# One float32r copy of the FFN weights, read in float16 through its upper halves

## The chip, the cores and the metric

The kernel runs on one core of one Trainium2 chip. The metric is the device time of one launch in microseconds (us). The kernel before was run three times; its median is 608.09 us (607.62 to 609.0).

## The reference

The input `x` has 8 batches of 512 tokens with 256 features. It is normalised, and then goes two ways: through attention with 16 heads of 16 features, rotary positions and a window of 250 tokens, and through a feed-forward network (FFN) whose weights are plus or minus one. The product of both is added to `x`.

```python
def _conn_dense(kernel_bool, x):
    w = jnp.where(kernel_bool, jnp.float32(1.0), jnp.float32(-1.0))
    return x @ w
...
h = jnp.concatenate([x, -x], axis=-1)
h = s0 * _conn_dense(k0, h)          # (512, 1024) booleans
h = jax.nn.relu(h) * 2
h = s1 * _conn_dense(k1, h)          # (1024, 1024) booleans
h = jax.nn.relu(h) * 2
h = s2 * _conn_dense(k2, h)          # (1024, 256) booleans
...
xn = _layernorm(x, axis=-1)
s = _L0_attn_ref(xn, L0_attn_in_proj_w, L0_attn_out_proj_w)
g = _silu(_L0_ffn_ref(xn, ...))
x = x + s * g
```

The first layer sees `x` and `-x`, so its two halves of weights fold into their difference, which is -2, 0 or 2 (in the kernel before, half of that: -1, 0 or 1).

## The kernel before

**Tiling.** Everything stands transposed: features on the 128 partitions, the 512 tokens of a batch along the free dimension. The 8 batches follow each other. In each, the FFN's first layer makes 8 tiles of 128 features from 2 chunks of input, the second makes 8 tiles from 8 chunks, the last makes 2 tiles from 8 chunks. Attention runs in 9 steps a batch, spread among the FFN's matmuls.

**Two parts of each activation.** Activations keep nearly float32's precision in two parts: `hi` is the value rounded to float16 (ScalarE, L307, L346, L529) and `lo` is what is left over, as float32r (VectorE, L305, L347, L527). A layer multiplies the weights with both and adds up in PSUM: first all chunks in float16, then all chunks in float32r (`of_both`, L514). For this the weights lie in SBUF twice, `w0`, `w1`, `w2` each with a part "h" (float16) and a part "l" (float32r), L158 to L164.

**Making the weights.** At the start the booleans come in as bytes (`kb0`, `kb1`, `kb2`). `make_w0h` subtracts the halves of `k0` (VectorE, L183), `make_w0l` copies that to float32r (ScalarE, L186), `make_w1` turns a slice of 128 output columns of `k1` into plus or minus a constant for one part (L188 to L194), on ScalarE or GpSimd. The constants carry the sign of the scale `s1`. `make_w2` does both parts on GpSimd (L196). The sizes of the three scales and the constants of the two powers of two are put right once at the end (`scales`, L200 to L207).

**Order.** The order of the work on each engine is written by hand. `everything` (L992) is a list of (time, cost, function); `run` (L226) sorts it by that planned time and issues the instructions so. Functions may return followers with a delay. Each engine then works through its instructions in that order and waits on semaphores for what it needs. The times of the weight slices stand in L1004 to L1010. DMA copies are issued from SP's queue, a few at the start from ScalarE's.

**q and k.** For the scores, q and k are projected, rotated (`rotate`, GpSimd, L425), split in a high half (ScalarE, L442) and a low half (VectorE, L449), written to DRAM (L435) and read back stacked (`stack`, L457). The scores are L733, their exponentials L752 (ScalarE), the masks L768 and L775 (GpSimd), the values L807. From batch 1 on the normalised `x` is made in transposed form: the moments go through DRAM (L281, L290), VectorE applies them (L301), ScalarE makes the high part `xh` (L307).

**Where weights are read.** `layer` (L502), with its matmul at L518, and `last` (L554), with its matmul at L572. A float16 matmul is two instructions on TensorE, a weight load and the matmul; a float32 or float32r one loads its weights itself, which shows as a load in the trace too.

The scale constants, and the reads in `layer`:

```python
X_SCALE, W1_SCALE = 2.0 ** 7, 2.0 ** -10
...
of_both = [(p, c) for p in "hl" for c in range(nc_in)]
...
    p, c = of_both[k]
    nc.tensor.matmul(
        ph, w[p][:, c, ts(f, P)], st[src + p][:, c, cols],
        start=(k == 0), stop=(k == n - 1),
    )
```

`plain_ffn` and all that stands under `tc.If(found < n_rows, label="general")` is a second way for inputs that the fast way can't take (a row with hardly any variance, a sum of exponentials out of range). It isn't entered with these inputs.

Of the kernel before, what the change touches and what calls it, by code (L numbers as in the profile page):

```python
# [23 lines left out]

LEAST, MOST = 1e-20, 1e30

LEAST_VAR = 1e-11

X_SCALE, W1_SCALE = 2.0 ** 7, 2.0 ** -10


@with_exitstack
def tile_attention_times_gated_ffn(
# [42 lines left out]
    nc = tc.nc  # L78
    P = 128
# [4 lines left out]
    EC = E // P  # L84
    F0, F1 = k0.shape[1], k1.shape[1]
# [7 lines left out]
    const = ctx.enter_context(tc.tile_pool(name="const", bufs=1))  # L93
# [23 lines left out]
    raw_pool = raw.enter_context(tc.tile_pool(name="raw", bufs=1))  # L117
# [11 lines left out]
    for n in (1, 0, 2):  # L129
# [26 lines left out]


    w0, w1, w2 = (  # L158
        {
            p: const.tile(shape, dt, name=f"w{i}{p}_sb")  # L160
            for p, dt in (("h", F16), ("l", F32R))
        }
        for i, shape in enumerate(([P, EC, F0], [P, NF0, F1], [P, NF1, E]))
    )  # L164

    sgn = const.tile([P, 3], F32, name="sgn")
    sgnx = const.tile([P, 1], F32, name="sgnx")
    sgn2 = const.tile([P, 3], F32, name="sgn2")
    sgnn = const.tile([P, 3], F32, name="sgnn")
# [15 lines left out]
    def make_w0l(c):  # L185
        nc.scalar.copy(w0["l"][:, c], w0["h"][:, c])  # L186

    def make_w1(f, p, engine):  # L188

        w, k = w1[p][:, :, ts(f, P)], kb1[:, :, ts(f, P)]  # L190
        if engine is nc.scalar:
            nc.scalar.activation(w, k, AF.Identity, bias=sgnn[:, 1:2], scale=sgn2[:, 1:2])
        else:
            engine.tensor_scalar(w, k, sgn2[:, 1:2], sgnn[:, 1:2], ALU.mult, ALU.add)  # L194

    def make_w2():  # L196
        for p in "hl":
            nc.gpsimd.tensor_scalar(w2[p], kb2, 2.0, -1.0, ALU.mult, ALU.add)

        mag = small.tile([P, 3], F32, tag="mag", name="mag")  # L200
        nc.vector.tensor_tensor(mag, s_sb[:, 0:3], sgn, ALU.mult)
        nc.vector.tensor_scalar(
            mag[:, 0:1], mag[:, 0:1], 8.0 / (X_SCALE * W1_SCALE), mag[:, 1:2],
            ALU.mult, ALU.mult,
        )
        nc.vector.tensor_tensor(scales[:, 0:1], mag[:, 0:1], s_sb[:, 2:3], ALU.mult)
        nc.vector.tensor_scalar(scales[:, 1:2], scales[:, 0:1], -1.0, None, ALU.mult)  # L207
# [294 lines left out]
    def layer(b, name, src, w, f, part=0, parts_=1, cols=slice(0, T)):  # L502

        st = states[b]
        nc_in = w["l"].shape[1]
        if f == 0 and part == 0 and cols.start == 0:
            for p, dt in (("h", F16), ("l", F32R)):
                st[name + p] = hpool.tile(
                    [P, NF0, T], dt, tag=f"{name}{p}", name=f"{name}{p}_{b}"
                )  # L510
        if part == 0:
            st["h"] = ps_m.tile([P, T], F32, tag="mm", name=f"h_ps_{b}_{f}")
        ph = st["h"][:, cols]
        of_both = [(p, c) for p in "hl" for c in range(nc_in)]  # L514
        n = len(of_both)
        for k in range(n * part // parts_, n * (part + 1) // parts_):
            p, c = of_both[k]
            nc.tensor.matmul(  # L518
                ph, w[p][:, c, ts(f, P)], st[src + p][:, c, cols],
                start=(k == 0), stop=(k == n - 1),  # L520
            )
# [32 lines left out]
    def last(b, u, how):  # L554
        st = states[b]
        f, cols = outputs(b)[u]
        if how == "final":
            pz = ps_s.tile([P, 2, T], F32, tag="sc", name=f"z_ps_{b}_{u}")[:, 0, : T // 2]
        else:
            pz = ps_m.tile([P, T], F32, tag="mm", name=f"z_ps_{b}_{u}")  # L560
            if b + 1 == B:
                pz = pz[:, : T // 2]
        if how == "at once":
            for c in range(NF1):
                nc.tensor.matmul(
                    pz, w2["l"][:, c, ts(f, P)].bitcast(F32), st["h2p"][:, c, cols],
                    start=(c == 0), stop=(c == NF1 - 1),
                )
        else:
            for p in "hl":  # L570
                for c in range(NF1):
                    nc.tensor.matmul(  # L572
                        pz, w2[p][:, c, ts(f, P)], st["h2" + p][:, c, cols],
                        start=(c == 0 and p == "h"), stop=(c == NF1 - 1 and p == "l"),
                    )
        if cols.start == 0:
            st["gate of", f] = outs.tile([P, T], F32, tag=f"gate{f}", name=f"gate_{b}_{f}")
        gate = st["gate", u] = st["gate of", f][:, cols]
        if how == "final":
            residual(b, u)  # L580
# [12 lines left out]

            return [(0.0, ends)]

        def scale():
            nc.vector.tensor_scalar(gate, pz, scales[:, 0:1], None, ALU.mult)
            if how != "later":
                return [(7.5 if u == 0 else 11.0, lambda: gate_ready(b, u))]

        return [(0.0, scale)]

    def plain_ffn(b):

        st = states[b]
        for name, src, w in (("h1p", "xp", w0["l"]), ("h2p", "h1p", w1["l"])):
# [391 lines left out]
    ]  # L998
    for c in range(EC):
        everything += [  # L1000
            (-34.4 if c == 0 else -32.8, 0, lambda c=c: make_w0h(c)),
            (-32.9 if c == 0 else -32.6, 0, lambda c=c: make_w0l(c)),
        ]
    for w, f, at, engine in (  # L1004
        ("l", 0, 4.6, nc.gpsimd), ("l", 1, 4.65, nc.gpsimd), ("l", 2, 10.2, nc.gpsimd),
        ("h", 0, -17, nc.scalar), ("h", 1, 8.6, nc.scalar), ("h", 2, 10.3, nc.gpsimd),
        ("l", 3, 11.8, nc.gpsimd), ("l", 4, 11.9, nc.gpsimd), ("l", 5, 12.0, nc.gpsimd),
        ("l", 6, 19.3, nc.gpsimd), ("l", 7, 19.4, nc.gpsimd), ("h", 3, 15.2, nc.scalar),
        ("h", 4, 17.0, nc.scalar), ("h", 5, 18.7, nc.scalar), ("h", 6, 20.4, nc.scalar),
        ("h", 7, 22.2, nc.scalar),  # L1010
    ):
        everything.append((at, 0, lambda f=f, w=w, e=engine: make_w1(f, w, e)))
    for b in range(B):
        everything += prepare(b) + ffn(b)
        for u in range(len(outputs(b))):
# [138 lines left out]
```

## Time and profile before

| what | us |
|---|---|
| median of 3 runs | 608.09 |
| the profiled execution | 606.75 |
| its span, first to last instruction | 605.0 |
| TensorE busy | 595.0 |
| VectorE busy | 382.6 |
| GpSimd busy | 310.6 |
| ScalarE busy | 294.6 |
| weight loads on TensorE (beside its matmuls) | 367.4 |

The busy shares by stage, in the answer by windows, one row a stretch:

```profile
core 0: us, PE busy (x) PEld busy (x) DVE busy (x) ACT busy (x) POOL busy (x), PEclk, DMA share, GB/s
0.00:15.00 15.00, 11.67 (x49) 9.40 (x50) 9.84 (x31) 6.04 (x11) 3.68 (x12) 1.00 0.86 267
15.00:40.00 25.00, 24.59 (x135) 15.49 (x137) 19.01 (x35) 19.15 (x27) 24.18 (x19) 1.00 0.67 233
40.00:60.00 20.00, 19.80 (x168) 9.77 (x160) 9.84 (x14) 11.44 (x14) 10.52 (x15) 1.00 0.24 84
60.00:80.00 20.00, 19.84 (x196) 11.88 (x188) 11.21 (x16) 11.68 (x14) 9.32 (x15) 1.00 0.78 273
80.00:200.00 120.00, 120.00 (x872) 71.19 (x871) 76.01 (x123) 58.55 (x81) 56.00 (x69) 1.00 0.30 99
```

A row gives the stretch, its length, then the busy time and number of instructions of TensorE's matmuls (PE), its weight loads (PEld), VectorE (DVE), ScalarE (ACT) and GpSimd (POOL), the granted TensorE clock, the busy share of the DMA engines and what they moved. From 15 to 40 us GpSimd is busy for 24.18 of 25 us and ScalarE for 19.15; there the weights are made. From 80 us on TensorE has a matmul in flight all the time. In groups of instructions, "L518 PEld LDWEIGHTS ... x576 | 51.2, 98" means: 576 weight loads of line 518, 51.2 us in all, 98 ns each on average. Matmuls are pipelined: one starts before the one ahead has ended, so the pace is read from starts, not from durations.

### The profile page before, as it was taken

How to read it: one execution, taken by the hardware profiler on the slowest of the kernel's cores; microseconds unless marked ns; L12 is line 12 of the kernel's file. 1: busy time of each engine (PE TensorE's matmuls, PEld its weight loads, DVE VectorE, ACT ScalarE, POOL GpSimd, SP SyncE). 2: the span in 40 equal slices, each digit the busy share in tenths (PEclk: the TensorE clock that was granted, in tenths of full speed). 3: DMA queues.
4: the chain of work that ended last, by engine and by line, in shares of the span. 5: the costliest groups of instructions: out<-in, count | busy, mean ns of one | idle time of the engine just before them, and what ended most of it. 6: DMA issues, size and time to landing. Idle time of an engine off the chain costs nothing. (4 is left out here: it accounts for less than half of the span.)

```text
span 605.0 us, 11181 instructions
## 1 busy us (share of the span) xinstructions
PE 595.0 (98%) x4492; PEld 367.4 (61%) x4492; DVE 382.6 (63%) x606; ACT 294.6 (49%) x414; POOL 310.6 (51%) x368
## 2 busy tenths in 40 slices
PE   7999999999999999999999999999999999999996
PEld 6654566555665556556566566655565556667785
DVE  6854647557576485665856658566676566645665
ACT  3776664444554535545354454543554435554422
POOL 2975532456623664436635457245572356536743
PEclk9999999999999999999999999999999999999998
DMA  8562822226331353315333252432524216212201
GB/s 268 219 192 87 280 88 89 87 83 231 106 120 56 134 180 105 123 53 205 109 105 123 92 211 75 145 110 85 209 91 135 89 70 224 91 53 71 89 1 38
DMA packets 38056, 74.46 MB, mean 123 GB/s; under 512 B 5360, under 2 KB 13040, under 8 KB 38000
## 3 DMA queue, kind: packets, MB, share of 16 engines
q1 hardware_dynamic: 35568, 71.48, 34.4%
q10 hardware_dynamic: 2432, 2.23, 1.2%
q8 instruction: 36, 0.59, 0.4%
q14 instruction: 20, 0.16, 0.1%
HBM read 44.30 MB, written 29.39 MB: 122 GB/s over the span
## 5 line engine op out<-in xcount | busy, mean ns | idle before, releaser
L752 ACT ACTIVATE p<-sc 128x1024 f32<-128x1024 f32 (+2 forms) x144 | 138.3, 1012 | 74.8 <-PE sc L733 44.9
L768 POOL TENSOR_SCALAR_AFFINE_SELECT p<-p 128x512 f32<-128x512 f32 x128 | 92.4, 727 | 126.3 <-ACT p L752 126.3
L518 PE MATMUL h_ps<-h1l,w1l_sb 128*128 128x512 f32 (+1 forms) x576 | 146.3, 396 | 0.0
L518 PE MATMUL h_ps<-h1h,w1h_sb 128*128 128x512 f16 (+1 forms) x576 | 123.1, 357 | 0.0
L518 PEld LDWEIGHTS h_ps<-h1l,w1l_sb 128*128 128x128 f32 x576 | 100.3, 188 | 29.4 <-issue 9.2
L529 ACT ACTIVATE h2h<-h_ps 128x512 f16<-128x512 f32 (+1 forms) x72 | 39.4, 548 | 113.2 <-PE h_ps L518 113.2
L518 PEld LDWEIGHTS <-w1h_sb 128*128 128x128 f16 x576 | 51.2, 98 | 58.8 <-issue 17.5
L775 POOL TENSOR_SCALAR_AFFINE_SELECT p<-p 128x512 f32<-128x512 f32 (+1 forms) x96 | 49.3, 514 | 72.6 <-ACT p L752 69.2
L807 PE MATMUL po<-p,v_pad 128*32 128x378 f32 (+4 forms) x1216 | 76.7, 372 | 0.1
L633 DVE RECIPROCAL den<-den 128x256 f32<-128x256 f32 (+1 forms) x32 | 52.5, 1644 | 24.9 <-POOL den L628 24.9
L527 DVE SCALAR_TENSOR_TENSOR h2l<-h_ps,h2h 128x512 fp32r<-128x512 f32 (+1 forms) x72 | 43.7, 608 | 30.5 <-ACT h2h L529 30.5
L733 PEld LDWEIGHTS sc<-q,k 32*128 32x128 f32 x1216 | 44.2, 184 | 30.4 <-issue 21.5
L527 DVE SCALAR_TENSOR_TENSOR h1l<-h_ps,h1h 128x512 fp32r<-128x512 f32 x64 | 42.7, 679 | 25.7 <-ACT h1h L529 25.6
L733 PE MATMUL sc<-q,k 32*128 32x378 f32 (+4 forms) x1216 | 58.1, 307 | 0.5 <-DMA q<-dq 0.3
L884 DVE RECIPROCAL S<-S 128x128 f32<-128x128 f32 x64 | 57.5, 920 | 0.1
L518 PE MATMUL h_ps<-xl,w0l_sb 128*128 128x512 f32 x128 | 52.3, 489 | 0.0
L807 PEld LDWEIGHTS po<-p,v_pad 128*32 128x32 f32 x1216 | 31.8, 109 | 28.7 <-issue 17.0
L529 ACT ACTIVATE h1h<-h_ps 128x512 f16<-128x512 f32 x64 | 38.0, 598 | 18.3 <-PE h_ps L518 18.3
L301 DVE TENSOR_TENSOR xT<-xT,of_all 128x512 f32<-128x512 f32 x28 | 22.1, 794 | 28.5 <-DMA of_all<-d 28.0
L518 PE MATMUL h_ps<-xh,w0h_sb 128*128 128x512 f16 x128 | 38.5, 382 | 0.1
L572 PE MATMUL z_ps<-h2l,w2l_sb 128*128 128x512 f32 (+1 forms) x144 | 36.1, 391 | 0.2 <-DVE h2l L527 0.2
L425 POOL TENSOR_TENSOR m_ka<-m_ka,m_kb 128x512 f32<-128x512 f32 x16 | 20.1, 1275 | 28.4 <-DVE m_kb L404 28.4
(101 smaller groups left out, 734.8 us busy)
## 6 DMA issues: line engine op xcount, KB each, us to landing
q<-dq SPq DMA_DIRECT2D x64, 256.0 KB, 3.3
dq<-qh SPq DMA_DIRECT2D x16, 512.0 KB, 3.1
dq<-m_qa SPq DMA_DIRECT2D x16, 512.0 KB, 5.3
k<-dk SPq DMA_DIRECT2D x32, 256.0 KB, 2.7
dk<-kh SPq DMA_DIRECT2D x8, 512.0 KB, 2.6
dk<-m_ka SPq DMA_DIRECT2D x8, 512.0 KB, 2.8
x<-in_x_dram SPq DMA_DIRECT2D x30, 128.0 KB, 2.9
xT<-in_x_t_dram SPq DMA_DIRECT2D x7, 512.0 KB, 5.5
```

Source lines behind the costliest of these rows:

```text
L301: nc.vector.tensor_tensor(xT, xT, st["of_all"][:, i], op)
L518: nc.tensor.matmul(ph, w[p][:, c, ts(f, P)], st[src + p][:, c, cols], start=(k == 0), stop=(k == n - 1),)
L527: nc.vector.scalar_tensor_tensor(lo, ph, 0.0, hi, ALU.max, ALU.subtract)
L529: high = lambda: nc.scalar.activation(hi, ph, AF.Relu)
L572: nc.tensor.matmul(pz, w2[p][:, c, ts(f, P)], st["h2" + p][:, c, cols], start=(c == 0 and p == "h"), stop=(c == NF1 - 1 and p == "l"),)
L633: nc.vector.reciprocal(part, part)
L733: nc.tensor.matmul(sc[r // 2][:, r % 2, ds(off, n)], st["k0", g][row, ts(j, P)], st[f"q{turn}", g][row, ds(j * P + first, n)], start=(turn ...
L752: nc.scalar.activation(p[:, 2 * half : 2 * half + 2, :n], sc[half][:, :, :n], AF.Exp, scale=D ** -0.5,)
L768: nc.gpsimd.affine_select(out=block, in_=block, compare_op=ALU.is_ge, fill=0.0, base=0, pattern=[[0, 4], [1, P]], channel_multiplier=-1,)
L775: nc.gpsimd.affine_select(out=block, in_=block, compare_op=ALU.is_ge, fill=0.0, base=-1, pattern=[[0, 4], [-1, beyond]], channel_multiplier=1,
L807: nc.tensor.matmul(po[32 * r : 32 * r + 32, ds(j * P + first, n)], v_columns(j, g, r), p_[:, r, ds(off, n)], start=(j == 0), stop=(done an ...
L884: nc.vector.reciprocal(part, part)
```

## The change

The weights are kept once, as float32r, with the values -2, 0 and 2. A float32 number of this size has zeros in its lower 16 bits, and its upper 16 bits read as float16 give the same number (2.0 is 0x40000000 in float32 and 0x4000 in float16). So the float16 matmuls read the float32r tile as a float16 tile of twice the width, and of it every second element: a view with a step of 2 elements (4 bytes) where the float16 copy had a step of 1.

With it:
- `make_kd0` (VectorE, in the place of `make_w0h`) writes the difference of `k0`'s halves to a float16 tile `kd0` in the pool of raw inputs; `make_w0` (ScalarE, in the place of `make_w0l`) writes it times two to `w0`.
- `make_w1` makes one slice for each f, 8 in place of 16. On ScalarE these are f = 0, 2, 6, 7 (before: 7 float16 slices), on GpSimd f = 1, 3, 4, 5 (before: 8 float32r slices and 1 float16 slice).
- `make_w2` makes one tile in place of two.
- Constants: `X_SCALE` is 2^-5 in place of 2^7, the scale of `w1` is 2 in place of 2^-10, and `LEAST_VAR`, the smallest variance that the fast way takes, 1e-7 in place of 1e-11.

In the built program TensorE, VectorE and SP have the same instructions in the same order as before, apart from tiles, steps and waits. The float16 copies took 24 KB of each partition; the buffers behind them move.

```diff
-X_SCALE, W1_SCALE = 2.0 ** 7, 2.0 ** -10
+X_SCALE = 2.0 ** -5
...
     w0, w1, w2 = (
-        {
-            p: const.tile(shape, dt, name=f"w{i}{p}_sb")
-            for p, dt in (("h", F16), ("l", F32R))
-        }
+        const.tile(shape, F32R, name=f"w{i}_sb")
         for i, shape in enumerate(([P, EC, F0], [P, NF0, F1], [P, NF1, E]))
     )
+
+    def weights(w, p, c, cols):
+        if p == "l":
+            return w[:, c, cols]
+        return w[:, c].bitcast(F16).rearrange("p (f two) -> p f two", two=2)[:, cols, 1]
...
-        nc.vector.tensor_scalar(sgn2, sgn, 2.0 * W1_SCALE, None, ALU.mult)
-        nc.vector.tensor_scalar(sgnn, sgn, -W1_SCALE, None, ALU.mult)
-
-    def make_w0h(c):
-
-        nc.vector.tensor_tensor(w0["h"][:, c], kb0[:, c], kb0[:, EC + c], ALU.subtract)
-
-    def make_w0l(c):
-        nc.scalar.copy(w0["l"][:, c], w0["h"][:, c])
-
-    def make_w1(f, p, engine):
-
-        w, k = w1[p][:, :, ts(f, P)], kb1[:, :, ts(f, P)]
+        nc.vector.tensor_scalar(sgn2, sgn, 4.0, None, ALU.mult)
+        nc.vector.tensor_scalar(sgnn, sgn, -2.0, None, ALU.mult)
+
+    kd0 = raw_pool.tile([P, EC, F0], F16, name="kd0")
+
+    def make_kd0(c):
+
+        nc.vector.tensor_tensor(kd0[:, c], kb0[:, c], kb0[:, EC + c], ALU.subtract)
+
+    def make_w0(c):
+        nc.scalar.mul(w0[:, c], kd0[:, c], 2.0)
+
+    def make_w1(f, engine):
+
+        w, k = w1[:, :, ts(f, P)], kb1[:, :, ts(f, P)]
...
     def make_w2():
-        for p in "hl":
-            nc.gpsimd.tensor_scalar(w2[p], kb2, 2.0, -1.0, ALU.mult, ALU.add)
+        nc.gpsimd.tensor_scalar(w2, kb2, 4.0, -2.0, ALU.mult, ALU.add)
...
-                ph, w[p][:, c, ts(f, P)], st[src + p][:, c, cols],
+                ph, weights(w, p, c, ts(f, P)), st[src + p][:, c, cols],
...
-                        pz, w2[p][:, c, ts(f, P)], st["h2" + p][:, c, cols],
+                        pz, weights(w2, p, c, ts(f, P)), st["h2" + p][:, c, cols],
...
-    for w, f, at, engine in (
-        ("l", 0, 4.6, nc.gpsimd), ("l", 1, 4.65, nc.gpsimd), ("l", 2, 10.2, nc.gpsimd),
-        ("h", 0, -17, nc.scalar), ("h", 1, 8.6, nc.scalar), ("h", 2, 10.3, nc.gpsimd),
-        ("l", 3, 11.8, nc.gpsimd), ("l", 4, 11.9, nc.gpsimd), ("l", 5, 12.0, nc.gpsimd),
-        ("l", 6, 19.3, nc.gpsimd), ("l", 7, 19.4, nc.gpsimd), ("h", 3, 15.2, nc.scalar),
-        ("h", 4, 17.0, nc.scalar), ("h", 5, 18.7, nc.scalar), ("h", 6, 20.4, nc.scalar),
-        ("h", 7, 22.2, nc.scalar),
+    for f, at, engine in (
+        (0, -17, nc.scalar), (1, 4.6, nc.gpsimd), (2, 8.6, nc.scalar),
+        (3, 10.2, nc.gpsimd), (4, 11.8, nc.gpsimd), (5, 11.9, nc.gpsimd),
+        (6, 15.2, nc.scalar), (7, 17.0, nc.scalar),
     ):
```

More of the change, by code (lines that the diff above doesn't have):

```diff
@@ L25 @@
 LEAST, MOST = 1e-20, 1e30
-LEAST_VAR = 1e-11
-X_SCALE, W1_SCALE = 2.0 ** 7, 2.0 ** -10
+LEAST_VAR = 1e-7
+X_SCALE = 2.0 ** -5
 @with_exitstack
@@ L202, in make_w2 @@
         nc.vector.tensor_scalar(
-            mag[:, 0:1], mag[:, 0:1], 8.0 / (X_SCALE * W1_SCALE), mag[:, 1:2],
+            mag[:, 0:1], mag[:, 0:1], 1.0 / X_SCALE, mag[:, 1:2],
             ALU.mult, ALU.mult,
@@ L504, in layer @@
         st = states[b]
-        nc_in = w["l"].shape[1]
+        nc_in = w.shape[1]
         if f == 0 and part == 0 and cols.start == 0:
@@ L565, in last @@
                 nc.tensor.matmul(
-                    pz, w2["l"][:, c, ts(f, P)].bitcast(F32), st["h2p"][:, c, cols],
+                    pz, w2[:, c, ts(f, P)].bitcast(F32), st["h2p"][:, c, cols],
                     start=(c == 0), stop=(c == NF1 - 1),
@@ L605, in plain_ffn @@
         st = states[b]
-        for name, src, w in (("h1p", "xp", w0["l"]), ("h2p", "h1p", w1["l"])):
+        for name, src, w in (("h1p", "xp", w0), ("h2p", "h1p", w1)):
             h = st[name] = hpool.tile(
@@ L1000, in tile_attention_times_gated_ffn @@
         everything += [
-            (-34.4 if c == 0 else -32.8, 0, lambda c=c: make_w0h(c)),
-            (-32.9 if c == 0 else -32.6, 0, lambda c=c: make_w0l(c)),
-        ]
-    for w, f, at, engine in (
-        ("l", 0, 4.6, nc.gpsimd), ("l", 1, 4.65, nc.gpsimd), ("l", 2, 10.2, nc.gpsimd),
-        ("h", 0, -17, nc.scalar), ("h", 1, 8.6, nc.scalar), ("h", 2, 10.3, nc.gpsimd),
-        ("l", 3, 11.8, nc.gpsimd), ("l", 4, 11.9, nc.gpsimd), ("l", 5, 12.0, nc.gpsimd),
-        ("l", 6, 19.3, nc.gpsimd), ("l", 7, 19.4, nc.gpsimd), ("h", 3, 15.2, nc.scalar),
-        ("h", 4, 17.0, nc.scalar), ("h", 5, 18.7, nc.scalar), ("h", 6, 20.4, nc.scalar),
-        ("h", 7, 22.2, nc.scalar),
+            (-34.4 if c == 0 else -32.8, 0, lambda c=c: make_kd0(c)),
+            (-32.9 if c == 0 else -32.6, 0, lambda c=c: make_w0(c)),
+        ]
+    for f, at, engine in (
+        (0, -17, nc.scalar), (1, 4.6, nc.gpsimd), (2, 8.6, nc.scalar),
+        (3, 10.2, nc.gpsimd), (4, 11.8, nc.gpsimd), (5, 11.9, nc.gpsimd),
+        (6, 15.2, nc.scalar), (7, 17.0, nc.scalar),
     ):
-        everything.append((at, 0, lambda f=f, w=w, e=engine: make_w1(f, w, e)))
+        everything.append((at, 0, lambda f=f, e=engine: make_w1(f, e)))
     for b in range(B):
```

## The prediction

> **What bounds the kernel now.** I read the page first (busy shares, then the costliest groups), then the groups of TensorE split by shape, then the timeline around the start and around single weight loads.
>
> ```profile
> PE 595.0 (98%) x4492; PEld 367.4 (61%) x4492; DVE 382.6 (63%) x606; ACT 294.6 (49%) x414; POOL 310.6 (51%) x368
> L518 PEld LDWEIGHTS h_ps<-h1l,w1l_sb 128*128 128x128 f32 x576 | 100.3, 188 | 29.4 <-issue 9.2
> L518 PEld LDWEIGHTS <-w1h_sb 128*128 128x128 f16 x576 | 51.2, 98 | 58.8 <-issue 17.5
> L807 PEld LDWEIGHTS po<-p,v_pad 128*32 128x32 f32 x1216 | 31.8, 109 | 28.7 <-issue 17.0
> ```
>
> TensorE is busy for 595.0 of 605.0 us; no other engine passes 63%. So what shortens another engine's work counts only where TensorE waits for it, and what lengthens TensorE's own pace counts in full. The last three lines are the weight loads in question: 98 ns for 128 float16 columns, 188 ns for 128 columns of 4 bytes, 109 ns for 32 columns of 4 bytes.
>
> ```profile
> L518 PE MATMUL h_ps<-h1h,w1h_sb 128*128 128x512 f16 x448 | 106.4, 381 | 0.0
> L518 PE MATMUL h_ps<-h1h,w1h_sb 128*128 128x256 f16 x128 | 16.7, 274 | 0.0
> ...
> 30.38 1.90 PE L518 MATMUL h_ps<-h1h,w1h_sb 128*128 128x512 f16 x8
> ...
> 114.24 0.55 PEld L518 LDWEIGHTS <-w1h_sb 128*128 128x128 f16 x4 [0.20 <-issue]
> 114.25 0.82 PE L518 MATMUL h_ps<-h1h,w1h_sb 128*128 128x512 f16 x3
> ...
> 580.32 1.05 PE L518 MATMUL h_ps<-h1h,w1h_sb 128*128 128x256 f16 x8
> 581.12 1.18 PE L518 MATMUL h_ps<-h1l,w1l_sb 128*128 128x256 f32 x8
> 582.14 1.05 PE L518 MATMUL h_ps<-h1h,w1h_sb 128*128 128x256 f16 x8
> ```
>
> Eight pipelined matmuls of 381 ns end after 1.90 us, so they start (1.90-0.381)/7 = 0.217 us apart; those of 256 columns (1.05-0.274)/7 = 0.111 us apart. (Row by row, start to start: 216 and 109 ns.) A float16 load of 98 ns fits beside either. Longer loads fit too: from 580.32 to 582.14, eight float16 and eight float32r matmuls take 1.82 us, so the float32r ones are (1.82-8x0.111)/8 = 0.117 us apart although each has a 188 ns load. The record of a load is longer than what it takes from the pace.
>
> The exception is the first load of a group: at 114.24 it starts with its matmul (114.25), not one matmul ahead. Row by row, 114 of the 848 float16 loads (576 at L518 for w1, 128 for w0, 144 at L572) start within 5 ns of their own matmul: the first after float32r or attention matmuls, not after the plain float32 projections. Such a first matmul holds the next one off by 226 ns instead of 216.
>
> The start of the program has the few waits:
>
> ```profile
> 17.98 2.37 POOL L194 TENSOR_SCALAR w1l_sb<-kb,sgn,sgnn 128x1024 fp32r<-128x1024 uint8 x2
> 20.32 3.48 POOL L425 TENSOR_TENSOR m_qa<-m_qa,m_qb 128x512 f32<-128x512 f32 x2
> 23.84 1.05 ACT L442 CAST qh<-m_qa 128x1024 fp32r<-128x1024 f32 x1 [1.07 <-POOL m_qa L425]
> 24.91 1.22 DVE L449 TENSOR_TENSOR m_qa<-m_qa,qh 128x1024 fp32r<-128x1024 f32 x1 [1.43 <-ACT qh L442]
> 34.83 0.62 PE L733 MATMUL sc<-q,k 32*128 32x378 f32 x12 [0.32 <-DMA q<-dq]
> 42.75 2.89 DVE L301 TENSOR_TENSOR xT<-xT,of_all 128x512 f32<-128x512 f32 x4 [2.25 <-DMA of_all<-d]
> 48.74 0.79 PE L733 MATMUL sc<-q,k 32*128 32x378 f32 x14 [0.20 <-ACT p L752]
> ```
>
> Read it as a chain: GpSimd makes two weight slices, then rotates q; ScalarE and VectorE wait for that; their halves go through DRAM; the first scores wait for the stacked q. From 34.07, where the first scores start, to the float16 matmuls at 35.38 is 1.31 us; the same 16 score matmuls take 0.72 us at 59.44. Stall: 0.59. At 48.10 they take 1.40, a stall of 0.68: they wait for ScalarE, whose exponentials stand behind the normalised x of batch 1, which waits for `of_all`, which queues on SP behind the q copies.
>
> [...]188-109 = 79 ns for 96 columns is 0.82 ns a column, so 83 ns of a record are fixed[...]. No row shows the strided form.[...]
>
> **The change, part by part.**
>
> *The steady stream.* The order on TensorE, VectorE and SP is that of before, instruction by instruction; only tiles and wait counts differ. Matmuls, columns and moving operands stay. 848 loads now read every second float16. Bounds: nothing at best (the packed load is the shortest record there is, so no gain), and at worst the 188 ns of a 4-byte load, 90 ns more. [...]about 12 ns more, a record of 110. For the 734 early loads that costs nothing: they start 108 ns (256 columns) or 214 ns (512) ahead, and the 188 ns loads started 115 ns ahead without cost. The 114 late ones pay: 114 x 12 ns = +1.4 us. At 90 ns they would pay 10.3 us.
>
> *w0.* ScalarE doubles a difference (ACTIVATE) where it cast one (CAST, 1.05 us at 10.92 and at 12.76). VectorE's subtraction stays. The float16 matmuls now wait for ScalarE's output, done at 13.81, 1.5 us before their first load at 15.28; up to 0.25 us more each is hidden there. VectorE's `xl` behind it may slip as much, and the rope products after it; the q product that matters runs at 18.05, behind `h1l`. Nothing.
>
> *w1 and w2, ScalarE.* Four slices instead of seven: 3 x 1.23 = 3.7 us less, at 32 to 39 us. The slice at 34.67 stood ahead of the first exponentials, but these need the scores anyway.
>
> *w1 and w2, GpSimd.* Four slices instead of nine and one w2 instead of two: 4 x 1.19 + 2.24 + 1.90 = 8.9 us less. Only one slice (1.19 us) goes from ahead of the q rotation: it starts when `m_qb` is there (VectorE, 18.05 + 1.28 = 19.33) instead of at 20.32, 1.0 us earlier. ScalarE is free by 22.77, so `qh`, VectorE's low half, the copies to and from DRAM all move by 1.0 us, and q lands in time: the stall of 0.59 at 34.07 goes. On SP the copies of the moments and `of_all` follow in the same queue and move by the same 1.0 us; so do the normalisation, ScalarE's two `xh` and the exponentials behind them. At 46.3 the last needs `h2h`, which TensorE gives 0.59 earlier. ScalarE then stands ahead by about 0.8 us at 48.1. What is late next is still ScalarE, so the start gives 0.8 us in all, not 0.59 + 0.68. Bounds: 0.3 (the copies are held by DMA traffic) and 1.6 (both stalls and the odd tenths after them). After 60 us TensorE is the bound, and carries that to the end.
>
> *Readiness of the single copy.* Each slice is now needed at the float16 half, about 1.6 us before the float32r half. On GpSimd f = 3 to 5 follow the rotation and end near 26.5; f = 3 is read at 40.76. On ScalarE f = 7 ends near 32.3 and is read after 70. No slice has under seven us of cover. The four scale constants, the smaller buffers and the new `kd0` (released with the raw booleans, last read before 14 us) cost nothing.
>
> *Sum.* +1.4 - 0.8 = +0.6 us. The profiled execution took 606.75 us, 605.0 of span and 1.75 around it: 607.35. It lies 1.34 under the median of 608.09, so against the median 608.7.
>
> **Rivals.** The smallest difference that a measurement of this kernel can tell from none is about 0.2%, 1.2 us.
>
> *The strided load is as short as the packed.* For: [...]a fixed part of 83 ns may hide the rest.[...] Then only the start moves: 608.09 - 0.8 = 607.3, and 606.5 at its bound.
>
> *The load loses its fast form (the slower side).* The place is the 114 late loads. The price is up to 90 ns each: 10.3 - 0.8 gives 617.6; half of it 612.4. It decides from a record of about 98 + (1.2+0.8)/114 = 116 ns on.[...]
>
> *The moving stream is slowed.* Float32r matmuls of 512 columns run at 0.234 (row by row) where float16 has 0.216, in proportion to their columns (0.117 against 0.109 at 256), so it is their stream that is slow, not their load. Were strided loads to do the same to 688 float16 matmuls of 512 and 160 of 256 columns, that is 688 x 0.018 + 160 x 0.008 = 13.7 us: 621.0. Against it: [...]plain float32 streams that bear 190 ns loads.
>
> **How the numbers follow.** Forecast 0.40 (most of it within 0.2%: same 0.24, slower 0.14, faster 0.02); load free 0.30 (faster 0.20, same 0.10); load slow 0.15; stream slowed 0.07; anything else, such as the moved buffers, 0.08 (half and half). Faster 0.26, same 0.34, slower 0.40. The range of the forecast alone is 606.9 to 610.2; down to 606.4 it takes in the free load with a start worth 1.6, up to 614 the lower half of the slow load. Left out: 0.05 of the slow load, the slowed stream, 0.06 below.
>
> **What would show it.** The float16 load's mean: 110 ns is the forecast, 98 the first rival, 188 the second. Pace of the float16 matmuls inside a group: still 0.216 and 0.109; 0.234 is the third. First matmul of a late group: 238 ns instead of 226. The q rotation on GpSimd near 19.3; the scores near 34 us without a wait for DMA; the next ones near 47 us with a shorter one for ScalarE. Wrong altogether, if TensorE waits anywhere for a weight slice, or if the stalls of the start come back later.

## The result, and the profile after

The changed kernel took 606.06 us (median of 14 runs, 605.48 to 606.77), before in the same session 607.06 (14 runs); the ratio is 0.9979, interval 0.9969 to 0.9989. Two more sessions, below, gave 606.56 beside 607.06 (0.9993, 0.9982 to 1.0004) and 606.32 beside 607.02 (0.9988, 0.9982 to 0.9995). The change makes the kernel about 0.7 us faster, 0.1%: (1.00 + 0.50 + 0.70)/3. The forecast was 608.7, 0.6 us slower. A ratio here is not the quotient of the two medians (it lies nearer to that of the means), so a difference of medians and its ratio can disagree by some hundredths of a per cent, which is as much as some of the effects below.

From the page of after: its line of engines, and three groups of its fifth part.

```profile
PE 594.7 (98%) x4492; PEld 367.3 (61%) x4492; DVE 381.1 (63%) x606; ACT 291.7 (48%) x411; POOL 302.9 (50%) x362
...
L521 PE MATMUL h_ps<-h1h,w_sb 128*128 128x512 f16 (+1 forms) x576 | 123.1, 357 | 0.0
L521 PEld LDWEIGHTS h_ps<-h1l,w_sb 128*128 128x128 f32 x576 | 100.2, 188 | 29.5 <-issue 9.2
L521 PEld LDWEIGHTS <-w_sb 128*128 128x128 f16 x704 | 61.1, 98 | 74.7 <-issue 29.1
```

The work on GpSimd fell to 302.9 us, by 7.7 where 8.9 had been foreseen. The last line settles the largest doubt: the float16 load, which now reads every second value, is still 98 ns long. Row by row the paces (0.216 and 0.109 us) and the time by which the first matmul of a late group holds the next one off (226 to 227 ns) are those of before as well.

The start, from the timelines of after (start, us taken, engine, line, operation, and in brackets what it waited for):

```profile
18.14 1.20 POOL L198 TENSOR_SCALAR w_sb<-kb,sgn,sgnn 128x1024 fp32r<-128x1024 uint8 x1
19.30 3.51 POOL L428 TENSOR_TENSOR m_qa<-m_qa,m_qb 128x512 f32<-128x512 f32 x2
22.83 1.05 ACT L445 CAST qh<-m_qa 128x1024 fp32r<-128x1024 f32 x1
23.91 1.72 SPq L438 DMA_DIRECT2D dq<-qh  x2
25.72 1.22 SPq L438 DMA_DIRECT2D dq<-m_qa  x2
29.79 1.82 SPq L460 DMA_DIRECT2D q<-dq  x2
34.81 0.62 PE L736 MATMUL sc<-q,k 32*128 32x378 f32 x12 [0.27 <-DMA q<-dq]
48.07 1.15 PE L736 MATMUL sc<-q,k 32*128 32x378 f32 x16
```

SP's copies of q in before:

```profile
24.91 0.80 SPq L435 DMA_DIRECT2D dq<-qh  x2
26.16 1.61 SPq L435 DMA_DIRECT2D dq<-m_qa  x2
30.23 2.07 SPq L457 DMA_DIRECT2D q<-dq  x2
```

One slice stands ahead of the q rotation instead of two, and the rotation starts at 19.30 instead of 20.32. SP issues the first store of q (`dq<-qh`) 1.0 us earlier too (23.91; before 24.91). But this issue takes 1.72 us instead of 0.80, the reload `q<-dq` starts only 0.44 us earlier, and the scores wait for q until 34.81, as before (34.83). Counted from TensorE's first matmul of the w0 layer (15.71 in before, 15.87 in after), the first store is issued 1.16 us earlier and the second reload, the one that lands just before those scores start, lands 0.19 us earlier (18.89 instead of 19.08). The rest of the lead, 0.97 us, is lost between that issue and the landing.

To see where the gain arises, the start of the same TensorE matmul is compared in the two traces. Worked out from the records, in us:

```
matmul                         before   after   lead of after
before the w0 layer             15.71   15.87   -0.16
first of the w1 layer           26.79   26.82   -0.03
first scores                    34.07   34.10   -0.03
after the scores of 48.1        49.51   49.19    0.32
scores of 64.5                  64.53   64.19    0.34
behind these                    65.60   65.39    0.21
scores of 69.1                  69.10   68.89    0.21
behind these                    70.04   69.62    0.42
float16 matmuls of 71           70.98   70.39    0.59
one near the end               592.08  591.48    0.60
```

After 71 us nothing moves. The first row is a warning: in the three profiles of after, one unchanged program, TensorE starts the w0 layer at 15.87, 15.59 and 16.50 us, so a single pair of profiles can differ here by as much as the whole gain. The lead comes out of a few waits, and three of them had not been foreseen: it loses 0.13 at 64.5, and gains 0.21 and 0.17 between 69 and 71. Whether each is of the change or of the execution, one profile cannot tell; the experiments had to.

### The profile page after: what moved, and what is told of

Read it like the earlier page. It is cut to its first block, busy times and chain, and to the rows that moved or that the text cites. A ratio compares the mean times of both kernels' runs of the same rounds, so it can differ in the third digit from the quotient of the medians.

```text
span 604.2 us, 11172 instructions
## 1 busy us (share of the span) xinstructions
PE 594.7 (98%) x4492; PEld 367.3 (61%) x4492; DVE 381.1 (63%) x606; ACT 291.7 (48%) x411; POOL 302.9 (50%) x362
## 5 line engine op out<-in xcount | busy, mean ns | idle before, releaser
L521 PE MATMUL h_ps<-h1l,w_sb 128*128 128x512 f32 (+1 forms) x576 | 146.1, 395 | 0.0
L521 PE MATMUL h_ps<-h1h,w_sb 128*128 128x512 f16 (+1 forms) x576 | 123.1, 357 | 0.0
L521 PEld LDWEIGHTS h_ps<-h1l,w_sb 128*128 128x128 f32 x576 | 100.2, 188 | 29.5 <-issue 9.2
L521 PEld LDWEIGHTS <-w_sb 128*128 128x128 f16 x704 | 61.1, 98 | 74.7 <-issue 29.1
L521 PE MATMUL h_ps<-xl,w_sb 128*128 128x512 f32 x128 | 52.3, 489 | 0.0
L521 PE MATMUL h_ps<-xh,w_sb 128*128 128x512 f16 x128 | 38.4, 382 | 0.1
L575 PE MATMUL z_ps<-h2l,w_sb 128*128 128x512 f32 (+1 forms) x144 | 36.0, 391 | 0.2 <-DVE h2l L530 0.2
```

The lines of the kernel that those rows point to most:

```text
L521: nc.tensor.matmul(ph, weights(w, p, c, ts(f, P)), st[src + p][:, c, cols], start=(k == 0), stop=(k == n - 1),)
L575: nc.tensor.matmul(pz, weights(w2, p, c, ts(f, P)), st["h2" + p][:, c, cols], start=(c == 0 and p == "h"), stop=(c == NF1 - 1 and p == "l"),)
```

## The experiments

### The view alone, and the making alone

reads_only keeps both copies and their making; the float16 matmuls read the upper halves of the float32r copy:

```diff
+    def weights(w, p, c, cols):
+        if p == "l":
+            return w["l"][:, c, cols]
+        return w["l"][:, c].bitcast(F16).rearrange("p (f two) -> p f two", two=2)[:, cols, 1]
...
-        nc.scalar.copy(w0["l"][:, c], w0["h"][:, c])
+        nc.scalar.mul(w0["l"][:, c], w0["h"][:, c], 2.0)
```

> Both copies are made in the order of before, by the same engines, with the values of two; the float16 matmuls read the float32r copy by the view, and the float16 copies of w1 and w2 are written and read by nobody. Theory 'start' (the whole gain comes from the fewer weight slices at the start, the view is free): the time of before, a ratio of 0.999 to 1.001; float16 loads 98 ns; TensorE reaches 48.4, 65 and 70 us where before does, within 0.15. Rival 'stream' (the view or the single copy makes the later stream better): a ratio of 0.997 to 0.999 with the start as before.

Measured: 606.99 us, 606.96 beside it, ratio 0.9995 (0.9985 to 1.0004). The group of its loads:

```profile
L523 PEld LDWEIGHTS <-w1l_sb 128*128 128x128 f16 x576 | 51.3, 98 | 58.8 <-issue 17.6
```

98 ns again; from 71 to 560 us it takes 489.10 us, before 489.12. After 71 us, where almost all of these loads stand, the view gives nothing and costs nothing. One expectation missed: TensorE does not reach the named places within 0.15 us of before, but 1.1 us later at 48 us and 0.55 at 65 and 70 us. 0.44 of that is there at its first matmul of the w0 layer (16.15); the rest comes and goes at the waits of 34 and 48 us.

making_only is the reverse: the changed making, with one packed tile as the weights of every float16 matmul.

```diff
+    flat = const.tile([P, P], F16, name="flat")
+    nc.gpsimd.memset(flat, 0.0625)
...
-        return w[:, c].bitcast(F16).rearrange("p (f two) -> p f two", two=2)[:, cols, 1]
+        return flat
```

> The weights are made as in the changed kernel, but every float16 matmul reads one packed tile of 128x128 that is filled once with 0.0625: what is left out is the float16 part's use of the weights. Theory 'start': the time of the changed kernel, a ratio to before of 0.997 to 0.999, loads 98 ns. Rival 'stream': the time of before, 0.999 to 1.001. If packed loads are still cheaper than strided ones where the trace can't show it, this is faster than the changed kernel by up to 1.4 us (114 late loads by 12 ns, the term of the prediction).

606.47 us, ratio 0.9991 (0.9983 to 0.9999), 489.09 us from 71 to 560. The two intervals overlap, so the times alone do not decide; together with the unchanged loads and paces they point to the making, or to what moves with it.

### What a longer load costs

The float16 loads of w1 take every fourth, then every eighth value (the columns are then others than the reference's).

```diff
+        if w is w1:
+            at = 4 * P * (cols.start // P % 4)
+            return w[:, c].bitcast(F16)[:, at + 1 : at + 4 * P : 4]
```

> The 576 float16 loads of w1 read every fourth float16 in place of every second (8 bytes apart), so they take other columns than the reference's. [...]record 98 ns, same time as the changed kernel.[...] 110 or more, and the first matmul of a late group above 226 ns.

> The same with every eighth float16 (16 bytes apart), other columns than the reference's. If distance never counts: 98 ns and the time of the changed kernel. [...]a record of 110 to 190 ns; the early loads still hide, the 76 late ones of w1 pay 1 to 7 us.

From the page of step8, the group that holds w1's 576 loads and w0's 128 ordinary ones:

```profile
L524 PEld LDWEIGHTS <-w_sb 128*128 128x128 f16 x704 | 84.3, 138 | 59.8 <-issue 30.8
```

Row by row, w1's loads are mostly 113 ns in step4 and 143 to 144 in step8, late or not. step4 took 607.34 us (1.0006, 0.9996 to 1.0016), step8 610.01 (1.0044, 1.0027 to 1.0060). In step4 TensorE leads before by 1.11 us at 71 us and by 0.01 at the end, lost in steps of 0.016 us, one at each late load of w1 (63 of the 114 late ones are w1's); in step8 a step is 0.047. Inside a group the paces stay 0.216 and 0.109 us in both. So only the late loads pay, and they pay what their record grows: 16 and 47 ns. That the prediction had right. But growth starts behind step 2: there the record is 98 ns, as for packed weights, and at step 4 it is 15 ns longer. So in both runs the second of the two outcomes named above came.

### Which part of the making

Three versions of after put a part of the removed making back, into tiles that nobody reads, beside after unaltered: one GpSimd slice ahead of the q rotation (slice_ahead), four behind it and a second w2 (behind_back), three ScalarE slices (scalar_back).

```diff
+    spare = const.tile([P, NF0, P], F32R, name="spare")
+    for f, at, engine in ((2, 4.65, nc.gpsimd),):
+        everything.append((at, 0, lambda f=f, e=engine: make_spare(f, e)))
...
+    for f, at, engine in ((5, 18.7, nc.scalar), (6, 20.4, nc.scalar), (7, 22.2, nc.scalar)):
```

> The changed kernel once more, unaltered, beside the three that follow. Both theories: 606.0 us, ratio 0.998. It is here for the spread of the places where before and after differ: in the first profile of after the block of 16 scores at 48.1 us took 1.13 us instead of 1.40, the stretch from 65.6 to 71.0 us was 0.38 us shorter, and the stall at the first scores (34.1 us) was as long as before. What comes again is of the kernel; what does not is of the execution.

> The changed kernel with one more slice of weights made by GpSimd ahead of the q rotation, into a tile that nobody reads, as before had it. Theory 'ahead' (the gain is the q rotation's lead): q rotation back at 20.3 us, the scores at 48.1 us back to 1.40 us, and 0.3 to 1.0 us of the gain of 1.0 gone: 606.4 to 607.0. Rival 'behind' (the gain is in what GpSimd no longer does after the rotation): q rotation back at 20.3 us all the same, the time stays at 606.0 to 606.2, and the stretch from 65.6 to 71.0 us stays 0.38 us shorter than in before.

> The changed kernel with the other GpSimd making put back behind the q rotation: four more slices and a second making of w2, into tiles that nobody reads. Theory 'ahead': the lead of the q rotation is kept (19.3 us), the scores at 48.1 us stay at 1.13 us, the time stays at 606.0 to 606.3. Rival 'behind': the mask of the sixth step waits 0.46 us again, the stretch from 65.6 to 71.0 us is 0.38 us longer, and the time is 606.4 to 607.0.

> The changed kernel with the three slices that ScalarE no longer makes put back at their former places, into a tile that nobody reads: 3.7 us of ScalarE in the first 65 us. Theories 'ahead' and 'behind': nothing comes back, 606.0 to 606.2. A third, 'scalar' (ScalarE's exponentials and evictions of the first steps come earlier because it makes less): the scores at 48.1 us or the stretch from 49 to 65 us grow by 0.2 to 1.0 us, 606.3 to 607.0.

Measured: 606.56, 606.75, 606.41 and 605.91 us (ratios in the table below). The block of scores at 48.1, 1.15 us in after's timeline, is back at 1.4 us in after_again and back at 1.13 in behind_back: it is of the execution. So is the wait for q at 34, where the stretch of the 16 scores ran from 0.7 to 2.3 us over all profiles. What repeats to 0.02 us is this:

- With one slice ahead of the q rotation the stretch from 15.71 to 26.79 us is 0.13 us shorter, with two it is not.
- The 0.38 us between 69 and 71 are gained in all four, so neither theory holds for them: 'behind' expected them back in behind_back.
- The scores at 64.5 wait for q in every kernel without ScalarE's last three slices, and not in scalar_back.

The last two lead to two engines that start late after a wait that has ended. A wait stands in the trace as a record (a row) of its own, so the time from its end to the start of the instruction behind it can be read.

### GpSimd's mask at 69 us

Timelines of before; ScalarE's exponentials, whose end the mask needs, and the mask:

```profile
66.94 1.90 ACT L752 ACTIVATE p<-sc 128x1000 f32<-128x1000 f32 x2 [1.75 <-PE po L807]
69.35 0.63 POOL L775 TENSOR_SCALAR_AFFINE_SELECT p<-p 128x512 f32<-128x512 f32 x1 [3.47 <-PE h_ps L518]
70.04 1.01 PE L807 MATMUL po<-p,v_pad 128*32 128x244 f32 x16
```

And of after:

```profile
66.73 1.90 ACT L755 ACTIVATE p<-sc 128x1000 f32<-128x1000 f32 x2 [1.52 <-PE po L810]
68.75 0.63 POOL L778 TENSOR_SCALAR_AFFINE_SELECT p<-p 128x512 f32<-128x512 f32 x1 [2.86 <-ACT p L755]
69.62 0.84 PE L810 MATMUL po<-p,v_pad 128*32 128x244 f32 x16
```

In before the exponentials end at 66.94 + 1.90 = 68.84, and the mask starts 0.51 us later; in after it starts 0.12 us later (68.63 to 68.75). The record of the mask's own wait ends 0.46 and 0.08 us before the mask. TensorE's products wait for the mask: in before it ends at 69.98 and they start at 70.04. (The bracket of the late line names a TensorE matmul: it ended during the pause, after the wait's record had ended.) The waits are the same in both programs; what differs is the number of the instruction in GpSimd's stream: among GpSimd's rows of the trace, counted from 0, the mask is row 68 in before and row 62 in after. Four kernels test the number against the work. Six or seven tiny memsets (one of 128x1 takes 0.10 us in before) shift the stream and add almost no work:

```diff
+    blank = const.tile([P, 1], F32, name="blank")
+    for _ in range(6):
+        nc.gpsimd.memset(blank, 0.0)
```

> The changed kernel with six tiny memsets on GpSimd in its idle time before 5 us, so that every later GpSimd instruction stands six places further back, as in before, with no work behind. Theory 'position' (the mask of the sixth step starts 0.46 us after its wait in before because of its place in GpSimd's instruction stream): the 0.46 us come back at 69 us, the stretch from 69.1 to 71.0 us is as in before (1.88 us instead of 1.50), 606.4 to 606.9. Rival 'making' (it is the weights' making that delays it): the mask starts 0.08 us after its wait, 1.50 us, 606.0 to 606.5.

> The kernel before with the same six memsets. 'Position': the mask moves off the place and starts 0.08 us after its wait, the stretch from 69.1 to 71.0 us falls from 1.88 to 1.50 us, 606.6 to 606.8, without any change to the weights. 'Making': 0.46 and 1.88 us, 607.0.

pool_back joins slice_ahead and behind_back, that is, all of GpSimd's former making:

> The changed kernel with all of GpSimd's former making put back into tiles that nobody reads: the slice ahead of the q rotation, four behind it, and a second w2; both the amount of making and the place in the stream are those of before. 'Position' and 'making' alike: 0.46 us and 1.88 us come back at 69 us; with the lead of the q rotation gone too, 606.9 to 607.2. If they do not come back, the difference comes from ScalarE's stream or from the tiles.

> The changed kernel with seven tiny memsets on GpSimd before 5 us, one more than in six_more, of which one stood in for a wait: the mask of the sixth step is now the instruction of the same number in GpSimd's stream as in before, without any of before's making. 'Place': it starts 0.46 us after its wait again, and the stretch from 69.1 to 71.0 us takes 1.88 us instead of 1.50; time 0.4 us over that of after. 'Making': 0.08 us and 1.50 us, the time of after.

Six memsets moved the mask by five only, since one took the place of a separate wait; six_more has number 67 and shows 0.08 us, so it told nothing about 68. The others do. The mask in before_six, then in seven_more:

```profile
69.56 0.63 POOL L778 TENSOR_SCALAR_AFFINE_SELECT p<-p 128x512 f32<-128x512 f32 x1 [3.06 <-ACT p L755]
```

```profile
69.01 0.63 POOL L781 TENSOR_SCALAR_AFFINE_SELECT p<-p 128x512 f32<-128x512 f32 x1 [3.32 <-PE h_ps L524]
```

before_six, with all the old making, has number 73 and 0.08 us; seven_more, with none of it, has number 68 and 0.46 us; so has pool_back. Numbers 62, 63, 67 and 73 are prompt, 68 is late, whatever is made. six_more and seven_more differ by one memset alone. The place decides, not the making.

### ScalarE's exponential at 55 us

The same, the other way round. Before, then after:

```profile
55.17 1.94 ACT L752 ACTIVATE p<-sc 128x1024 f32<-128x1024 f32 x2 [2.54 <-PE po L807]
56.99 1.05 ACT L442 CAST kh<-m_ka 128x1024 fp32r<-128x1024 f32 x1
```

```profile
55.19 1.94 ACT L755 ACTIVATE p<-sc 128x1024 f32<-128x1024 f32 x2 [2.87 <-PE po L810]
57.01 1.05 ACT L445 CAST kh<-m_ka 128x1024 fp32r<-128x1024 f32 x1
...
65.13 0.33 PE L736 MATMUL sc<-q,k 32*128 32x128 f32 x4 [0.15 <-DMA q<-dq]
```

TensorE leads by 0.32 us here, so ScalarE's wait ends at 54.81 instead of 55.13; yet the exponential starts at the same time, 0.38 us after its wait (0.05 in before). The cast of k stands behind it, then the stores and reloads of k and q on SP (`q<-dq` is issued at 60.60, in before at 60.58), and at 65.13 the scores wait for q. In after's records a second such start comes 256 records later (the waits are rows 62 and 318 of ScalarE, at 54.77 and 367.14 us; the exponentials behind them start 382 and 328 ns after the waits end). All its other starts after an idle wait come 0.04 to 0.05 us behind it, but for one of 0.13 us at 593 us, which before has too, and the loading of a table at 5 us (1.28 us).

To part the place from the work, three one-column copies at 14 us stand in for three slices: into a new tile (scalar_three), or of a column of w0 onto itself (scalar_self).

```diff
+    blank = const.tile([P, 1], F32, name="blank")
+    for _ in range(3):
+        everything.append((-32.5, 0, lambda: nc.scalar.copy(blank, w0[:, 0, 0:1].bitcast(F32))))
...
+        everything.append((-32.5, 0, lambda: nc.scalar.copy(w0[:, 0, 0:1], w0[:, 0, 0:1])))
```

> The changed kernel with three one-column copies on ScalarE in its idle time near 14 us, so that all later ScalarE instructions have the same numbers in its stream as in before, with 0.1 us of work in place of 3.7. 'Place': the exponential at 55 us starts 0.05 us after its wait instead of 0.38, the k rotation's transfers and q come 0.33 us earlier, the scores at 64.5 us don't wait for q, the stretch from 64.5 to 65.6 us takes 1.0 to 1.1 us instead of 1.2 to 1.65; 605.6 to 606.2. 'Making' (less ScalarE work is what moves it): 0.38 us and the time of after.

> The changed kernel unaltered, a third time, beside the two others, for its median and the spread of the three places: 606.0 to 606.6, and 0.38 us at ScalarE's exponential at 55 us, 0.08 us at GpSimd's mask at 69 us.

> The changed kernel with three one-column copies on ScalarE near 14 us, of a column of w0 onto itself, and no new tile. 'Place' (of the instruction in ScalarE's stream): the exponential at 55 us starts 0.05 us after its wait, no wait for q at 64.5 us, 605.7 to 606.2; the stretch from 71 to 560 us as in after. 'Address' (of the tiles, for the 0.9 us between 71 and 560 us): this one does not have them. If the 0.9 us are there, the instructions bring them.

The timelines of scalar_self:

```profile
54.76 1.94 ACT L755 ACTIVATE p<-sc 128x1024 f32<-128x1024 f32 x2 [2.54 <-PE po L810]
...
64.13 1.25 PE L736 MATMUL sc<-q,k 32*128 32x244 f32 x24
```

The start is prompt again (54.71 to 54.76), and no wait for q is named, with 0.6 us of copies in place of 3.7 us of slices: again the place. (The block from 64.13 still took 1.18 us instead of 1.0 to 1.1.) scalar_self took 605.78 us (0.9981, 0.9972 to 0.9991). scalar_three took 604.99, a gain much larger than the place is worth; the rest lay between 71 and 560 us.

### A tile of 32 bytes

tile_only has scalar_three's tile, written once by GpSimd, without the ScalarE copies:

```diff
+    blank = const.tile([P, 1], F32, name="blank")
+    nc.gpsimd.memset(blank, 0.0)
```

> The changed kernel with the 32-byte tile of scalar_three at the same address, written once by GpSimd before 5 us, and no ScalarE instruction more. 'Address': the float32r matmuls of h1l and h2l are again 1.6 to 2.7 ns closer, 0.9 us shorter between 71 and 560 us; the exponential at 55 us starts 0.38 us after its wait as in after; 605.2 to 605.7. Otherwise: as after, 606.0 to 606.6.

605.35 us (0.9967, 0.9956 to 0.9977). Two groups of the page of after, whose matmuls stream h1l and h2l:

```profile
L521 PE MATMUL h_ps<-h1l,w_sb 128*128 128x512 f32 (+1 forms) x576 | 146.1, 395 | 0.0
L575 PE MATMUL z_ps<-h2l,w_sb 128*128 128x512 f32 (+1 forms) x144 | 36.0, 391 | 0.2 <-DVE h2l L530 0.2
```

And of tile_only:

```profile
L521 PE MATMUL h_ps<-h1l,w_sb 128*128 128x512 f32 (+1 forms) x576 | 145.4, 394 | 0.0
L575 PE MATMUL z_ps<-h2l,w_sb 128*128 128x512 f32 (+1 forms) x144 | 35.7, 389 | 0.1
```

The tile moves all later tiles by 32 bytes in each partition. h1l goes from 126304 to 126336, a multiple of 64; w1, at 28736, is one already. Only where both are (tile_only and scalar_three) do these matmuls come closer, start to start: by 1.6 ns for h1l and 2.5 for h2l, which is 0.91 of the 0.94 us gained from 71 to 560. In six_more, seven_more and before_six h1l lies on a multiple and the weights no longer do: no gain (489.16 to 489.23). It is not a rule for every such matmul: those of xl with w0, where both are multiples too, came only 0.4 ns closer. In before h1l also lies 32 over a multiple, so the change itself brought nothing here.

### The lead of the q rotation once more

q_first moves the last slice ahead of the q rotation behind it:

```diff
-        (0, -17, nc.scalar), (1, 4.6, nc.gpsimd), (2, 8.6, nc.scalar),
+        (0, -17, nc.scalar), (1, 10.1, nc.gpsimd), (2, 8.6, nc.scalar),
```

> The changed kernel with its last slice ahead of the q rotation moved behind it, so that the q rotation starts at 18.1 us instead of 19.3. Theory 'ahead': a further 0.13 us before 26.8 us, and q lands before the scores at 34 us, so the block of 16 scores there takes 0.84 us instead of 1.27 to 1.75: 605.4 to 605.8. Rival 'transfer' (what q waits for is the transfers queued together between 24 and 31 us, not the rotation): the block at 34 us stays at 1.1 to 1.8 us, 605.9 to 606.6.

606.59 us, ratio 1.0003 (0.9994 to 1.0012). Its timelines:

```profile
19.47 2.51 POOL L428 TENSOR_TENSOR m_qa<-m_qa,m_qb 128x512 f32<-128x512 f32 x2 [0.96 <-DVE m_qb L407]
20.73 2.34 DVE L452 TENSOR_TENSOR m_ka<-m_ka,kh 128x1024 fp32r<-128x1024 f32 x1
23.72 0.59 PE L521 MATMUL h_ps<-xh,w_sb 128*128 128x512 f16 x2 [1.08 <-DVE h1l L530]
24.31 0.81 SPq L438 DMA_DIRECT2D dq<-qh  x2
31.23 1.51 SPq L460 DMA_DIRECT2D q<-dq  x2
35.43 0.79 PE L736 MATMUL sc<-q,k 32*128 32x378 f32 x16
```

The rotation, whose second half runs beside VectorE's low half of k, now takes 2.51 us instead of the 3.51 of after, and VectorE's operation takes 2.34 us instead of 1.30. `h1l` comes late, and TensorE waits 1.08 us for it: 0.98 us lost against after before 26.8 us. The scores of 35.43 don't wait for q, but that does not support 'ahead': the rotation starts at 19.47, not at the 18.1 expected, the store and the reload of q are issued at 24.31 and 31.23 us (after: 23.91 and 29.79), and counted from TensorE's first w0 matmul the second reload lands no earlier than in after (18.97 and 18.89 us). q is in time because TensorE comes a microsecond later. 'Ahead' and 'transfer' stay undecided. In either order one of the two operations takes about 1 us longer than in the other (1.00 us on GpSimd, 1.04 on VectorE); why, no run here shows.

### All together

Before stands with the median of the session of after_third. The start delays are read row by row; "ahead" counts the GpSimd slices ahead of the q rotation.

| kernel | median us | minus median of before | ratio (interval) | ahead | ScalarE at 55, us | GpSimd at 69, us | 71 to 560, us |
|---|---|---|---|---|---|---|---|
| before | 607.02 | | | 2 | 0.05 | 0.46 | 489.12 |
| after | 606.06 | -1.00 | 0.9979 (0.9969-0.9989) | 1 | 0.38 | 0.08 | 489.09 |
| after_again | 606.56 | -0.50 | 0.9993 (0.9982-1.0004) | 1 | 0.38 | 0.08 | 489.10 |
| after_third | 606.32 | -0.70 | 0.9988 (0.9982-0.9995) | 1 | 0.38 | 0.08 | 489.10 |
| slice_ahead | 606.75 | -0.31 | 1.0001 (0.9991-1.0010) | 2 | 0.38 | 0.08 | 489.09 |
| behind_back | 606.41 | -0.65 | 0.9987 (0.9981-0.9994) | 1 | 0.38 | 0.08 | 489.10 |
| six_more | 606.56 | -0.39 | 0.9999 (0.9989-1.0009) | 1 | 0.38 | 0.08 | 489.17 |
| pool_back | 607.24 | +0.29 | 1.0012 (1.0003-1.0020) | 2 | 0.38 | 0.46 | 489.11 |
| before_six | 606.72 | -0.23 | 0.9994 (0.9986-1.0003) | 2 | 0.05 | 0.08 | 489.23 |
| seven_more | 606.85 | -0.17 | 0.9996 (0.9988-1.0005) | 1 | 0.38 | 0.46 | 489.16 |
| scalar_back | 605.91 | -1.15 | 0.9978 (0.9970-0.9987) | 1 | 0.05 | 0.08 | 489.09 |
| scalar_self | 605.78 | -1.26 | 0.9981 (0.9972-0.9991) | 1 | 0.05 | 0.08 | 489.10 |
| tile_only | 605.35 | -1.69 | 0.9967 (0.9956-0.9977) | 1 | 0.38 | 0.08 | 488.15 |
| scalar_three | 604.99 | -2.03 | 0.9967 (0.9954-0.9979) | 1 | 0.05 | 0.08 | 488.14 |

No pair of neighbours is told apart by its times, with intervals of a tenth of a per cent to either side. Four terms, chosen after these runs had been seen, were fitted to the differences of medians, weighted by their numbers of runs, with reads_only and making_only added and q_first, where other things moved too, left out. They give, with standard errors: one slice fewer ahead of the q rotation -0.56 (0.13) us, ScalarE's late start +0.38 (0.10), GpSimd's prompt one -0.48 (0.12), the shifted tiles -1.01 (0.21). The last three agree with what the profiles show of them: 0.33, 0.38 and 0.94. The first rests on five kernels with two slices ahead. In their profiles the stretches that begin at 34 and 48 us take 1.65 and 1.32 us on average, against 1.46 and 1.12 in the eleven other kernels of the fit: 0.2 us more in each, which with the 0.13 would make 0.5, but each of the two differences has a standard error of 0.15 to 0.2 us. The change carries the first three terms: -0.56 + 0.38 - 0.48 = -0.66 us. scalar_three, after with three tiny copies and a tile of 32 bytes, was the fastest, by 2 us on before.

## Why the prediction was wrong

**The step that failed** is the term "The 114 late ones pay: 114 x 12 ns = +1.4 us". That the late loads alone pay was right, as step4 and step8 show (0.016 and 0.047 us each). The 12 ns were not right: where "a record of 110" was foreseen, 98 ns were measured, 0 instead of +1.4 us. The 12 ns were the author's estimate; no float16 load in before's trace was strided, so nothing there showed it. Without the term the forecast's sum is -0.8 us, near the measured -0.7: this is the first rival, which had 0.30.

**The start**, "-0.8": the q rotation did move by 1.0 us. "q lands in time: the stall of 0.59 at 34.07 goes" failed: the wait is there in after and after_again, the first store's issue takes 1.72 us instead of 0.80, the reload starts 0.44 us earlier and not 1.0, and what is left at the landing is 0.19 us. From issue to landing the first store's copies took 3.7 us, in before 3.1, and the reloads 4.4 and 3.8 (medians between 22 and 36 us); why, no run isolates. One profile could not size the lead; by the fit it is worth about 0.56 us, of which 0.13 before 26.8 us repeat in each profile. The rest is argued from the fit, not shown in a place. The 19.3 of the rotation came true for another reason than the one given: the slice left ahead of it ends at 19.33, while `m_qb`'s second half ends only at 19.48, and q_first, without that slice, starts the rotation soon after the first half. Of the stall at 48.1, 0.28 us were gone in after, but in after_again they were not; the prediction read one execution's wait there as the kernel's.

**What it had at nothing** were the removed ScalarE and GpSimd instructions after 30 us. Their work cost nothing, as it said. Their number mattered: fewer instructions ahead moved one start on ScalarE into a pause and one on GpSimd out of one, +0.38 and -0.48 by the fit. These nearly cancel, so that -0.7 is not a proof of the start's -0.8.

**Right**: the early loads cost nothing (from 71 to 560 us 489.09 us, in before 489.12), the paces are unchanged (0.216 and 0.109 us), no matmul waits for a weight slice, and after 71 us nothing follows.

**The range**, 606.4 to 614.0, missed 606.06 by 0.3 us. It hung on a median of 608.09 from three runs; those three and eleven more runs of before gave 607.06. The one profiled execution of before, 606.75 us, lay nearer to that. The first rival's -0.8 from there is 606.3. The low end should have taken in that three runs can lie 1 us off.

## What to carry to other kernels

- Before you price a changed access by its bytes, measure one: float16 weight loads at step 2 took the same 98 ns as packed ones, those at steps 4 and 8 took 113 and 143 to 144. If no row of the trace shows the access, give "no change" the larger chance.
- Taking instructions away moves all that follow in that engine's stream. At this size, check two programs for constant late starts after a wait (here 0.38 us on ScalarE, 0.46 on GpSimd), and test with empty instructions before crediting the work removed. The same goes for tile addresses (here 0.94 us).
- A lead that passes through DMA copies need not be kept one to one (here 1.16 us at the first store, 0.19 at the landing); read a wait on them from several executions.

## What had not been expected of the hardware

- A start right after a wait was 0.33 to 0.46 us late at one number of GpSimd's stream (the mask's row 68) and two of ScalarE's (the waits' rows 62 and 318), whatever the instructions ahead do. ScalarE's two lie 256 rows apart. The page of after lists two DMA queues of the kind "instruction". The 16 KB packets of the one with 36 (0.59 MB) all run 2 us or more away from these late starts, in every profile. Of the other's, an 8 KB packet starts 0.26 to 1.31 us after ScalarE's row 62 in all 19 profiles, in those where the start is late and in those where no wait stands there. So a packet of that queue goes with ScalarE's first place; what causes the pauses no run here shows.
- Float32r matmuls of 512 columns in two of three groups came 1.6 and 2.5 ns closer when the stream and its weights both began at multiples of 64 bytes, in the third 0.4 ns; which of the moved tiles decides was not tried.
- Float16 weight loads of 128 x 128 took 98 ns packed and at step 2, 113 at step 4 and 143 to 144 at step 8, against 188 for 4-byte values.
